# Reordering the opening of a conditional adapter with layer norm

## The chip, the cores and the metric

One core of one Trainium2 chip. The metric is the device time of one launch in microseconds (us).

## The reference

For each of 128 batches x is 128 x 512 in float32, and an index names one of 10 languages with its own weights:

```python
h = relu(einsum('bsh,bha->bsa', x, W1[id]) + b1[id])       # 512 -> 128
y = x + einsum('bsa,bah->bsh', h, W2[id]) + b2[id]          # 128 -> 512
normed = (y - mean(y)) * rsqrt(var(y) + 1e-5)
out = x + normed * gamma[id] + beta[id]
```

## The kernel before

A batch is one tile, 128 rows on the partitions. x is loaded in groups of four batches, in the opening in pairs (`load_part`, L86). For each batch:

- TensorE transposes x in four blocks (`transpose_x`, L264, the matmuls at L271), into one PSUM buffer; ScalarE copies them to SBUF (`copy_xT`, L273).
- TensorE multiplies with W1 (`down`, L290, eight half-matmuls at L294); ScalarE applies b1 and relu (`relu`, L300). Batches 0 to 16 get their W1 by a load of their own into a staging buffer (`load_first`, L158, pool `wp`); later ones get it from the resident `w1` by a ScalarE copy (`stage_w1`, L259). The resident `w1` arrives in four pieces of 640 KB (`load_w1`, L101).
- TensorE multiplies with W2 (`up`, L304, at L311) into one of five PSUM buffers (pool `p_y`). W2 is resident, loaded in two pieces.
- b2 is added in one of three ways. By TensorE, as a product of a picked row ahead of `up` (L310, batches in `b2_by_matmul`). By VectorE, in place (`vector_b2`, L318, batches in `b2_by_vector`). Else by GpSimd (POOL), which makes x + b2 ahead of time (`add_b2`, L277).
- VectorE adds x and sums (`residual`, L323), ScalarE squares and sums (`square`), small steps give the reciprocal deviation, VectorE scales by gamma (`scale`) and adds x + beta (`finish`, L399), which POOL has made ahead of time in the output buffer (`add_beta`, L283, pool `op`). SP stores two batches at a time (`store`).

The rows of beta, gamma and b2 must stand on all 128 partitions. There are 30 of them, numbered 0 to 9 for beta, 10 to 19 for gamma, 20 to 29 for b2. Each is dealt out in one of two ways: `spread` (L225), a TensorE product with a picked column and a ScalarE copy, or `shuffle_rows` (L244), a VectorE shuffle out of one tile that holds all of them. `spin` (L518) issues TensorE products whose result is not used.

The order on each engine is written out by hand: `keep` chains each instruction to the one before it on its engine. SP's queue issues the loads in the order written at L167 to L202. The opening is the list at L533 to L574, and the loop over `i` behind it takes the batches from there.

Of the kernel before, what the change touches and what calls it, by code (L numbers as in the profile page):

```python
# [26 lines left out]
def cond_resid_kernel(ctx: ExitStack, tc: tile.TileContext, x, itok, W1, b1, W2, b2, gamma, beta, out):  # L27
# [8 lines left out]
    nc = tc.nc  # L36
    B, S, H = x.shape
# [8 lines left out]
    def keep(ins):  # L46

        engine = ins.ins.engine
        if engine in last:
            tc.add_manual_dep(ins.ins, last[engine], behind, reason="kept order")  # L50
        last[engine] = ins.ins.name
        return ins
# [1 line left out]
    const = ctx.enter_context(tc.tile_pool(name="const", bufs=1))  # L54
    xp = ctx.enter_context(tc.tile_pool(name="xp", bufs=4))
    rp = ctx.enter_context(tc.tile_pool(name="rp", bufs=4))
    op = ctx.enter_context(tc.tile_pool(name="op", bufs=8))
    tp = ctx.enter_context(tc.tile_pool(name="tp", bufs=2))
    wp = ctx.enter_context(tc.tile_pool(name="wp", bufs=7))
    st = ctx.enter_context(tc.tile_pool(name="st", bufs=6))  # L60
    p_x = ctx.enter_context(tc.tile_pool(name="p_x", bufs=1, space=PSUM))
    p_h = ctx.enter_context(tc.tile_pool(name="p_h", bufs=1, space=PSUM))
# [4 lines left out]
    E = B - 5  # L67
# [18 lines left out]
    def load_part(lo, hi, engine=nc.sync):  # L86
        dst = xs[lo // G][:, lo % G : lo % G + hi - lo, :]
        keep(engine.dma_start(out=dst, in_=x[lo:hi].rearrange("b s h -> s b h")))
# [12 lines left out]
    def load_w1(k):  # L101
        keep(
            nc.sync.dma_start(out=w1[:, :, k, :], in_=W1[:, k * P : (k + 1) * P, :].rearrange("l p a -> p l a"))
        )
# [35 lines left out]
    def lid(b, engine):  # L140
        g = b // G
        if (g, engine) not in lids:
            loads, vals = nc.values_load_multi_w_load_instructions(
                lang[0:1, g * G : (g + 1) * G],
                engines=[engine],
                min_val=0,
                max_val=L - 1,
                skip_runtime_bounds_check_because="clamped on the chip to 0..L-1 above",
            )
            for ins in loads:  # L150
                keep(ins)
            lids[g, engine] = vals
        return lids[g, engine][b % G]
# [4 lines left out]
    def load_first(b):  # L158
        w1s[b] = wp.tile([P, KC, A], FP, tag="w1s", name=f"w1s_{b}")
        src = W1[bass.ds(lid(b, ET.SP), 1)].rearrange("o (p k) a -> p (o k a)", k=KC)  # L160
        keep(nc.sync.dma_start(out=w1s[b].rearrange("p k a -> p (k a)"), in_=src))  # L161
# [13 lines left out]
    load_part(4, 6)  # L175
    load_first(4)
    load_first(5)
    load_part(6, 8)
    load_first(6)
    load_first(7)  # L180
    xs[2] = xp.tile([P, G, H], FP, tag="x", name="x_2")
    load_part(8, 10)
    load_first(8)
    load_first(9)
    load_part(10, 12)
    load_first(10)
    load_first(11)
    xs[3] = xp.tile([P, G, H], FP, tag="x", name="x_3")
    load_part(12, 14)
    load_first(12)  # L190
    load_w1(0)
    load_first(13)
    load_part(14, 16)
    load_first(14)
    load_w1(1)
    load_first(15)
    xs[4] = xp.tile([P, G, H], FP, tag="x", name="x_4")
    load_part(16, 18)
    load_w1(2)
    load_first(16)  # L200
    load_part(18, 20)
    load_w1(3)  # L202

    def upper(lo):

# [19 lines left out]
    def spread(r, copier):  # L225
        t = (beta_b, gamma_b, b2_b)[r // L]
        row = p_y.tile([P, H], FP, tag="y", name=f"row_{r}")
        pick_r = pick[:, r : r + 1].to_broadcast([96, P])
        keep(nc.tensor.matmul(row, lhsT=pick_r, rhs=parts[:96, :], start=True, stop=True))  # L229
        dst = t[:, r % L * H : (r % L + 1) * H]  # L230
        if copier is nc.scalar:
            keep(nc.scalar.copy(dst, row))
        else:
            keep(nc.vector.tensor_copy(dst, row))
# [9 lines left out]
    def shuffle_rows(lo, hi):  # L244
        for r in range(lo, hi):
            t = (beta_b, gamma_b, b2_b)[r // L]
            keep(nc.vector.stream_shuffle(t[:, r % L * H : (r % L + 1) * H], fours[0], [r] * 32))  # L247
# [3 lines left out]


    def b2_by_matmul(b):
        return b in (0, 1) or b >= B - 2

    def b2_by_vector(b):
        return b in (2, 3, 9, 13, 17, 21) or 24 <= b < B - 8 and (b % 16 in (1, 6, 11) or b % 32 == 30)

    def stage_w1(b):  # L259
        w1s[b] = wp.tile([P, KC, A], FP, tag="w1s", name=f"w1s_{b}")  # L260
# [22 lines left out]
    def add_beta(b):  # L283
        g, j = divmod(b, 2)
        if j == 0:
            os[g] = op.tile([P, 2, H], FP, tag="o", name=f"o_{g}")
        v = lid(b, ET.Pool)
        keep(nc.gpsimd.tensor_tensor(os[g][:, j, :], xb(b), beta_b[:, bass.ds(v * H, H)], ALU.add))  # L288
# [15 lines left out]
    def up(b):  # L304
        v = lid(b, ET.PE)
        ys[b] = p_y.tile([P, H], FP, tag="y", name=f"py_{b}")
        m = b2_by_matmul(b)
        if m:
            pick_b = pick[:, bass.ds(v + 2 * L, 1)].to_broadcast([96, P])
            keep(nc.tensor.matmul(ys[b], lhsT=pick_b, rhs=parts[:96, :], start=True, stop=False))  # L310
        keep(nc.tensor.matmul(ys[b], lhsT=hT[b], rhs=w2[:, bass.ds(v * H, H)], start=not m, stop=True))  # L311
        del hT[b]
# [97 lines left out]
    def on(b):  # L410
        return 0 <= b < B
# [106 lines left out]
    def spin(n, width):  # L518
        idle = p_s.tile([P, H], FP, tag="s", name="idle")
        for _ in range(n):  # L520
            keep(
                nc.tensor.matmul(
                    idle[:, :width], lhsT=ones, rhs=ones[:, 0:1].to_broadcast([P, width]), start=True, stop=True
                )
            )
# [3 lines left out]
    def x_turn(b):  # L529
        transpose_x(b)  # L530
        copy_xT(b)
# [1 line left out]
    spin(7, H)  # L533
    four_copies()
    spread(10, nc.scalar)
    spin(1, H)
    x_turn(0)
    transpose_b1()
    spread(11, nc.scalar)
    for n in (0, G):  # L540
        lid(n, ET.PE)
    shuffle_rows(0, 10)
    x_turn(1)
    spread(12, nc.scalar)
    spread(13, nc.scalar)
    down(0)
    relu(0)
    spread(14, nc.scalar)
    x_turn(2)
    spread(15, nc.scalar)  # L550
    down(1)
    relu(1)
    spread(16, nc.scalar)
    spread(17, nc.scalar)
    x_turn(3)
    down(2)
    relu(2)
    spread(18, nc.scalar)
    spread(19, nc.scalar)
    add_beta(0)  # L560
    add_beta(1)
    spread(20, nc.scalar)
    spread(21, nc.scalar)
    down(3)
    relu(3)
    spread(22, nc.scalar)
    add_beta(2)
    add_beta(3)
    shuffle_rows(23, 30)
    spin(1, H)  # L570
    spin(1, H // 2)
    up(0)
    x_turn(4)
    up(1)  # L574

    turned = 5
    for i in range(3, B + U):
        b = i - U - 1
        if b > G and b % G == 2 and b // G + 3 < NG and b // G + 3 >= 5:
            load_x(b // G + 3)  # L580
        up_to = i
        if b <= E:
            if turned <= up_to and on(turned):
                transpose_x(turned)
            add_b2(b + 2)
            if 4 <= b + 2 <= E:
                add_beta(b + 2)
        for n in range(turned, min(B, up_to) + 1):
            if on(n) and (n > turned or b > E):
                transpose_x(n)  # L590
            down(n - 1)
            if on(n):
                copy_xT(n)
            relu(n - 1)
            if on(n + 1) and n + 1 >= FIRST:
                stage_w1(n + 1)
        turned = max(turned, min(B, up_to) + 1)
        if i - U >= 2 and on(i - U):
            up(i - U)

        g, half = divmod(b, 2)
        p = g - 1
        mine, old = 0 <= p < B // 2, 0 <= p - 1 < B // 2
        if b == E:
            add_b2(b + 3)
            add_beta(b + 1)
            add_b2(b + 4)
            for n in range(b + 2, B):
                add_beta(n)
        if b > E:  # L610
            tail(b)
        elif half == 0:
            if on(b):
                vector_b2(b)
                residual(b)
                square(b)
            if mine:
                scale(2 * p)
                rstd(p, 1)
            if old:  # L620
                finish(2 * p - 1)
                store(p - 1)
        else:
            if on(b):
                vector_b2(b)
            if mine:
                rstd(p, 2)
            if on(b):
                residual(b)
                square(b)  # L630
            if mine:
                rstd(p, 3)
                scale(2 * p + 1)
            if mine:
                finish(2 * p)
        if 0 <= g and b <= E and half == 1:
            scalar_means(g)
            deviation(g)

        for n, engine in ((turned + 2, ET.Activation), (i - U + 3, ET.PE), (b + 1, ET.DVE), (b + 6, ET.Pool)):  # L640
            if on(n):
                lid(n, engine)
# [37 lines left out]
```

## Time and profile before

| what | us |
|---|---|
| median of 3 runs | 304.56 (304.44 to 304.68) |
| the profiled execution | 304.08 |
| its span | 302.3 |
| TensorE (PE) busy | 290.6 |
| VectorE (DVE) busy | 294.2 |
| ScalarE (ACT) busy | 279.6 |
| GpSimd (POOL) busy | 284.9 |

Times in the trace count from the start of the span. PEld is TensorE's weight load, SP the engine that issues most DMAs. Matmuls are pipelined: the distance from start to start tells more than the length shown.

### The profile page before, as it was taken

What the parts mean: (1) busy time and instruction counts of PE and PEld (TensorE: products, weight loads), DVE (VectorE), ACT (ScalarE), POOL (GpSimd) and SP (SyncE); (2) the same over time, 40 slices, a digit from 0 to 9 for tenths busy, and PEclk for the clock granted to TensorE, in tenths of its full rate; (3) what the DMA queues carried; (4) which work ended last, traced back from release to release, by engine and by line L of the source; (5) the groups of instructions that cost most, each with busy time, mean ns of one, the idle gap of its engine ahead of it and who ended that gap; (6) DMA issues with size and microseconds to landing.
All of it is one profiled execution on the core that took longest, in us unless ns stands there. A gap on an engine that the chain in (4) does not pass through costs nothing.

```text
span 302.3 us, 7001 instructions
## 1 busy us (share of the span) xinstructions
PE 290.6 (96%) x1820; PEld 218.0 (72%) x1821; DVE 294.2 (97%) x784; ACT 279.6 (92%) x771; POOL 284.9 (94%) x240
## 2 busy tenths in 40 slices
PE   7899999999999999999999999999999999999980
PEld 3758787777777777777777777777777777777740
DVE  6989999999999999999999999999999999999995
ACT  5878789999999999999999999999999999999982
POOL 1299998999999999999999999999999999999995
PEclk9999999999999999999999999999999999999997
DMA  6999999986667876766678667767866666882244
GB/s 235 385 389 364 346 339 402 404 307 206 233 234 243 279 255 205 244 209 261 222 280 270 212 204 240 263 226 261 279 211 221 218 253 217 271 283 113 108 166 173
DMA packets 43929, 77.33 MB, mean 256 GB/s; under 512 B 2121, under 2 KB 8020, under 8 KB 43890
## 3 DMA queue, kind: packets, MB, share of 16 engines
q1 hardware_dynamic: 43254, 76.31, 73.5%
q10 hardware_dynamic: 636, 0.57, 0.6%
q8 instruction: 15, 0.25, 0.3%
q14 instruction: 24, 0.20, 0.2%
HBM read 43.32 MB, written 33.55 MB: 254 GB/s over the span
## 4 chain that ended last, share of the span: by engine, by line
PE 89%; DVE 5%; DMA 2%; issue 1%; ACT 1%; SPq 0%; POOL 0%; DVEq 0%; ACTq 0%; POOLq 0%
PE ph L294 36%; PE py L311 35%; PE pxT L271 18%; DMA x<-in_x_dram 2%; DVE py L394 2%; DVE py L328 1%; DVE o L403 1%; PE row L229 1%; SPq L161 0%; ACT n L450 0%; ACT sq L351 0%; ACT sq L436 0%; DVE o L461 0%; ACT w1s L262 0%; DVE rstd L370 0%
## 5 line engine op out<-in xcount | busy, mean ns | idle before, releaser
L288 POOL TENSOR_TENSOR o<-x,beta_b 128x512 f32<-128x512 f32 x128 | 170.1, 1359 | 12.7 <-DVE beta_b L247 11.6
L294 PE MATMUL ph<-xT,w1s 128*128 128x128 f32 x1024 | 135.3, 275 | 0.2 <-DMA w1s<-in_L_cond_W_dram 0.2
L281 POOL TENSOR_TENSOR r<-x,b_b 128x512 f32<-128x512 f32 x97 | 131.7, 1360 | 0.0
L311 PE MATMUL py<-w,hT 128*128 x256 | 131.3, 595 | 0.0
L294 PEld LDWEIGHTS ph<-xT,w1s 128*128 128x128 f32 x1024 | 124.8, 192 | 1.3 <-issue 0.6
L271 PEld LDWEIGHTS pxT<-ident,x 128*128 128x128 f32 x512 | 66.0, 149 | 66.8 <-issue 49.9
L394 DVE SCALAR_TENSOR_TENSOR py<-py,nmean,gamma_b 128x512 f32<-128x512 f32 x126 | 94.8, 753 | 0.0
L403 DVE SCALAR_TENSOR_TENSOR o<-py,rstd,o 128x512 f32<-128x512 f32 x122 | 91.1, 747 | 0.0
L351 ACT ACTIVATE sq<-py,sum 128x512 f32<-128x512 f32 x124 | 85.8, 692 | 0.6 <-DVE py L328 0.6
L275 ACT COPY xT<-pxT 128x512 f32<-128x512 f32 x128 | 74.7, 583 | 4.3 <-PE pxT L271 4.1
L271 PE MATMUL pxT<-ident,x 128*128 128x128 f32 x512 | 77.6, 274 | 0.8 <-DMA x<-in_x_dram 0.6
L262 ACT COPY w1s<-w 128x512 f32 x111 | 68.0, 613 | 0.0
L328 DVE SCALAR_TENSOR_TENSOR py<-py,r 128x512 f32<-128x512 f32 x97 | 66.9, 690 | 0.2
L302 ACT ACTIVATE hT<-ph,b1T 128x128 f32<-128x128 f32 x128 | 46.9, 367 | 8.8 <-PE ph L294 4.2
L311 PEld LDWEIGHTS py<-w,hT 128*128 128x128 f32 x256 | 39.1, 192 | 1.4 <-issue 0.7
L351 ACT ACTIVATION_READ_ACCUMULATOR sq<-py,sum 128x1 f32 x124 | 25.1, 202 | 0.0
L328 DVE SCALAR_TENSOR_TENSOR py<-py,x 128x512 f32<-128x512 f32 x31 | 21.7, 699 | 1.4 <-PE py L311 1.1
L321 DVE TENSOR_TENSOR py<-py,b_b 128x512 f32<-128x512 f32 x27 | 18.6, 689 | 0.1
L361 ACT ACTIVATE root<-ssq,eps 128x2 f32<-128x2 f32 x62 | 16.5, 265 | 0.0
L328 DVE DVE_READ_ACCUMULATOR py<-py,r 128x1 f32 x97 | 13.6, 140 | 0.0
L342 ACT ACTIVATE nmean<-sum 128x2 f32<-128x2 f32 x62 | 12.3, 198 | 0.0
L365 DVE SCALAR_TENSOR_TENSOR part<-ssq,root 128x2 f32<-128x2 f32 x62 | 9.3, 149 | 0.2 <-ACT root L361 0.2
(57 smaller groups left out, 81.2 us busy)
## 6 DMA issues: line engine op xcount, KB each, us to landing
out_dram<-o SPq DMA_DIRECT2D x61, 512.0 KB, 3.3
x<-in_x_dram SPq DMA_DIRECT2D x27, 1024.0 KB, 6.7
x<-in_x_dram SPq DMA_DIRECT2D x10, 512.0 KB, 7.2
w1s<-in_L_cond_W_dram SPq DMA_DIRECT2D x17, 256.0 KB, 8.7
w<-in_L_cond_W_dram SPq DMA_DIRECT2D x4, 640.0 KB, 8.2
w<-in_L_cond_W_dram SPq DMA_DIRECT2D x1, 1792.0 KB, 9.8
w<-in_L_cond_W_dram SPq DMA_DIRECT2D x1, 768.0 KB, 5.3
out_dram<-o SPq DMA_DIRECT2D x3, 256.0 KB, 2.0
```

The costliest lines, as they stand in the source:

```text
L262: keep(nc.scalar.copy(w1s[b].rearrange("p k a -> p (k a)"), src))
L271: keep(nc.tensor.transpose(pxs[b][:, k, :], cols, ident))
L275: keep(nc.scalar.copy(xT[b], pxs.pop(b)))
L281: keep(nc.gpsimd.tensor_tensor(rs[b], xb(b), b2_b[:, bass.ds(v * H, H)], ALU.add))
L288: keep(nc.gpsimd.tensor_tensor(os[g][:, j, :], xb(b), beta_b[:, bass.ds(v * H, H)], ALU.add))
L294: nc.tensor.matmul(phs[b], lhsT=w1s[b][:, k, :], rhs=xT[b][:, k, :], start=(k == 0), stop=(k == KC - 1))
L302: keep(nc.scalar.activation(hT[b], phs.pop(b), AF.Relu, bias=b1T[:, bass.ds(lid(b, ET.Activation), 1)]))
L311: keep(nc.tensor.matmul(ys[b], lhsT=hT[b], rhs=w2[:, bass.ds(v * H, H)], start=not m, stop=True))
L328: nc.vector.scalar_tensor_tensor(ys[b], ys[b], 1.0, r, ALU.mult, ALU.add, accum_out=col(sums, b))
L351: nc.scalar.activation(sq, ys[b], AF.Square, bias=col(sums, b), scale=-float(H), accum_out=col(ssqs, b))
L394: nc.vector.scalar_tensor_tensor(ys[b], ys[b], col(nmeans, b), gamma_b[:, bass.ds(v * H, H)], ALU.add, ALU.mult)
L403: nc.vector.scalar_tensor_tensor(o, ys.pop(b), rstds[g][:, j : j + 1], o, ALU.mult, ALU.add)
```

## The change

Six things are changed.

- In the opening `up(0)` and `up(1)` stand together, ahead of the transposes of batch 4. Before, those stood between them.
- Batch 0 gets its b2 by VectorE and no longer by TensorE; of batches 9 and 10, batch 10 now gets it by VectorE and 9 by POOL.
- The 30 rows are dealt out anew: before, beta by shuffles, gamma by spreads; now both kinds are mixed, with 14 spreads in place of 13 and 16 shuffles in place of 17. The idle products stand elsewhere, three wide and two half ones in place of two wide and one half one, besides the first seven.
- `add_beta` of batches 0 to 4 is issued in the opening, at other places.
- The loads behind W2 stand in another order. `load_first(6)` is ahead of x of 6 and 7; the first piece of the resident `w1` comes right behind that, ahead of `load_first(7)`; and so on.
- The pool `wp` has five buffers in place of seven, the pool `op` nine in place of eight.

```diff
-    op = ctx.enter_context(tc.tile_pool(name="op", bufs=8))
+    op = ctx.enter_context(tc.tile_pool(name="op", bufs=9))
-    wp = ctx.enter_context(tc.tile_pool(name="wp", bufs=7))
+    wp = ctx.enter_context(tc.tile_pool(name="wp", bufs=5))
...
     load_part(4, 6)
     load_first(4)
     load_first(5)
+    load_first(6)
     load_part(6, 8)
-    load_first(6)
+    load_w1(0)
     load_first(7)
+    load_first(8)
     xs[2] = xp.tile([P, G, H], FP, tag="x", name="x_2")
     load_part(8, 10)
-    load_first(8)
+    load_part(10, 12)
     load_first(9)
-    load_part(10, 12)
-    load_first(10)
-    load_first(11)
+    load_w1(1)
     xs[3] = xp.tile([P, G, H], FP, tag="x", name="x_3")
     load_part(12, 14)
+    load_first(10)
+    load_part(14, 16)
+    load_first(11)
     load_first(12)
-    load_w1(0)
-    load_first(13)
-    load_part(14, 16)
-    load_first(14)
-    load_w1(1)
-    load_first(15)
     xs[4] = xp.tile([P, G, H], FP, tag="x", name="x_4")
     load_part(16, 18)
+    load_first(13)
     load_w1(2)
+    load_first(14)
+    load_first(15)
     load_first(16)
+    load_w1(3)
     load_part(18, 20)
-    load_w1(3)
...
     def b2_by_matmul(b):
-        return b in (0, 1) or b >= B - 2
+        return b in (1,) or b >= B - 2
     def b2_by_vector(b):
-        return b in (2, 3, 9, 13, 17, 21) or ...
+        return b in (0, 2, 3, 10, 13, 17, 21) or ...
...
     spread(10, nc.scalar)
-    spin(1, H)
+    shuffle_rows(9, 10)
+    spread(0, nc.scalar)
     x_turn(0)
     transpose_b1()
...
     relu(3)
-    spread(22, nc.scalar)
+    shuffle_rows(26, 27)
+    spread(28, nc.scalar)
+    spread(16, nc.scalar)
+    spread(18, nc.scalar)
+    shuffle_rows(27, 28)
+    up(0)
+    shuffle_rows(21, 22)
+    shuffle_rows(25, 26)
+    shuffle_rows(20, 21)
+    up(1)
+    x_turn(4)
     add_beta(2)
     add_beta(3)
-    shuffle_rows(23, 30)
-    spin(1, H)
-    spin(1, H // 2)
-    up(0)
-    x_turn(4)
-    up(1)
+    add_beta(4)
+    shuffle_rows(24, 25)
```

More of the change, by code (lines that the diff above doesn't have):

```diff
@@ L253, in b2_by_matmul @@
     def b2_by_matmul(b):
-        return b in (0, 1) or b >= B - 2
+        return b in (1,) or b >= B - 2
     def b2_by_vector(b):
-        return b in (2, 3, 9, 13, 17, 21) or 24 <= b < B - 8 and (b % 16 in (1, 6, 11) or b % 32 == 30)
+        return b in (0, 2, 3, 10, 13, 17, 21) or 24 <= b < B - 8 and (b % 16 in (1, 6, 11) or b % 32 == 30)
     def stage_w1(b):
@@ L535, in cond_resid_kernel @@
     spread(10, nc.scalar)
-    spin(1, H)
+    shuffle_rows(9, 10)
+    spread(0, nc.scalar)
     x_turn(0)
     transpose_b1()
-    spread(11, nc.scalar)
+    shuffle_rows(5, 6)
+    spin(1, H)
     for n in (0, G):
         lid(n, ET.PE)
-    shuffle_rows(0, 10)
+    shuffle_rows(4, 5)
+    shuffle_rows(6, 7)
+    shuffle_rows(2, 3)
+    spread(17, nc.scalar)
+    spread(1, nc.scalar)
     x_turn(1)
-    spread(12, nc.scalar)
-    spread(13, nc.scalar)
+    spread(11, nc.scalar)
     down(0)
     relu(0)
-    spread(14, nc.scalar)
+    shuffle_rows(13, 14)
+    spread(3, nc.scalar)
+    spread(12, nc.scalar)
+    shuffle_rows(7, 8)
+    spread(8, nc.scalar)
+    add_beta(0)
+    add_beta(1)
     x_turn(2)
-    spread(15, nc.scalar)
+    spin(2, H)
+    spin(1, H // 2)
+    shuffle_rows(14, 15)
     down(1)
     relu(1)
-    spread(16, nc.scalar)
-    spread(17, nc.scalar)
+    shuffle_rows(29, 30)
+    spin(1, H // 2)
+    shuffle_rows(23, 24)
+    spread(15, nc.scalar)
     x_turn(3)
@@ L557, in cond_resid_kernel @@
     relu(2)
-    spread(18, nc.scalar)
+    spread(22, nc.scalar)
     spread(19, nc.scalar)
[L560 to L563, printed above, removed]
     down(3)
     relu(3)
-    spread(22, nc.scalar)
+    shuffle_rows(26, 27)
[9 more added lines that the diff above has]
+    x_turn(4)
     add_beta(2)
     add_beta(3)
-    shuffle_rows(23, 30)
-    spin(1, H)
-    spin(1, H // 2)
-    up(0)
-    x_turn(4)
-    up(1)
+    add_beta(4)
+    shuffle_rows(24, 25)
     turned = 5
@@ L580, in cond_resid_kernel @@
             load_x(b // G + 3)
-        up_to = i
+        up_to = i + {}.get(i, 0)
         if b <= E:
@@ L585, in cond_resid_kernel @@
             add_b2(b + 2)
-            if 4 <= b + 2 <= E:
+            if 5 <= b + 2 <= E:
                 add_beta(b + 2)
```

## The prediction

> **What bounds the kernel now.** I read the page first, then TensorE's time by stretches, its timeline where the change sits, and last the landings of the loads.
>
> ```profile
> span 302.3 us, 7001 instructions
> PE 290.6 (96%) x1820; PEld 218.0 (72%) x1821; DVE 294.2 (97%) x784; ACT 279.6 (92%) x771; POOL 284.9 (94%) x240
> PE 89%; DVE 5%; DMA 2%; issue 1%; ACT 1%; SPq 0%; POOL 0%; DVEq 0%; ACTq 0%; POOLq 0%
> 20.00:25.00 5.00, 5.00 (x34) 4.06 (x33) 4.88 (x14) 4.39 (x14) 5.00 (x5) 1.00 1.05 384
> 100.00:150.00 50.00, 50.00 (x321) 37.88 (x320) 49.93 (x131) 49.01 (x140) 50.00 (x42) 1.00 0.73 244
> ```
>
> Four engines are nearly full, so busy shares do not choose between them. The chain that ended last does: 89% of it is PE. In the stretches (length, busy time of PE, PEld, DVE, ACT and POOL, granted clock, DMA share, GB/s) PE has no gap from 20 us on. So whatever moves PE's unbroken stretch moves the end by as much, if the others keep up. The second reading is the DMA share: 1.05 at 20 to 25 us against 0.73 later. In the opening the DMA engines have no slack either, and there the order of the loads is the order of their landing. The span is 302.3 us in an execution of 304.08 us; the median of the runs shown is 304.56. I take differences inside the profiled execution and add them to the median.
>
> **The products up of 0 and 1.** I call the four transposes of a batch its turn (L271), L294 its product down, L311 its product up. PE's timeline (start, length) around the exchanged steps, the wait in it, and ACT's copy of turn 4:
>
> ```profile
> 16.15 0.38 PE L310 MATMUL py<-parts,pick 96*128 96x512 bf16 x1
> 16.37 1.10 PE L311 MATMUL py<-w,hT 128*128 x2
> 17.47 0.75 PE L271 MATMUL pxT<-ident,x 128*128 128x128 f32 x4
> 18.05 0.38 PE L310 MATMUL py<-parts,pick 96*128 96x512 bf16 x1
> 18.27 1.88 PE L311 MATMUL py<-w,hT 128*128 x4
> 19.99 0.63 PE L271 MATMUL pxT<-ident,x 128*128 128x128 f32 x4
> 20.46 1.06 PE L294 MATMUL ph<-xT,w1s 128*128 128x128 f32 x8
> 21.35 1.02 PE L311 MATMUL py<-w,hT 128*128 x2
> PEld pxT L271 <- DMA x<-in_x_dram: 0.8, 1, 0.8
> 18.31 0.59 ACT L275 COPY xT<-pxT 128x512 f32<-128x512 f32 x1 [1.53 <-PE pxT L271]
> ```
>
> By starts (lengths are pipelined) a product up takes (19.99 - 18.27) / 2 = 0.86, the b2 row ahead of it 16.37 - 16.15 = 0.22, a turn 20.46 - 19.99 = 0.47, but 18.05 - 17.47 = 0.58 when it had to wait for its data, since its weight loads are then not hidden. Turn 4 waited for x of batch 4. Now up(0), without a row, stands there: it starts between 16.15 and 16.37, and I take 16.20. Then 0.86, row 1 with 0.22, up(1) 0.86, turn 4 0.47, up(2) 0.86 give 19.47 for turn 5. But turn 5 also needs the copy of turn 4, which started 18.31 - 17.47 = 0.84 after the turn and took 0.59: 18.14 + 1.43 = 19.57. Against 19.99 that gains about 0.40, with ends at 0.25 and 0.55. If nothing else stood in the way, that would be the result.
>
> **b2 of batch 0, the rows, POOL.**
>
> ```profile
> 19.40 0.70 DVE L328 SCALAR_TENSOR_TENSOR py<-py,x 128x512 f32<-128x512 f32 x1 [1.08 <-PE py L311]
> 13.10 4.98 POOL L288 TENSOR_TENSOR o<-x,beta_b 128x512 f32<-128x512 f32 x4 [11.64 <-DVE beta_b L247]
> 91.01 0.75 DVE L403 SCALAR_TENSOR_TENSOR o<-py,rstd,o 128x512 f32<-128x512 f32 x1
> 91.81 1.12 PE L311 MATMUL py<-w,hT 128*128 x2
> ```
>
> VectorE's new addition for batch 0 costs about 0.70, like its neighbours, and fits into its 1.08 idle ahead of residual(1): nothing. Moving the vector batch from 9 to 10 is not quite free. VectorE falls behind by one such step and recovers within the next batches; one place later, it begins 13, 17 and 21 a little later. At 91 us the cover is gone already: finish ends at 91.01 + 0.75 = 91.76, and the product up that takes the freed buffer begins at 91.81 and lasts 1.12 instead of 1.02. I take another 0.10 there, bounds 0 and 0.25.
>
> POOL idled 11.64 for the beta rows; with rows 0, 1, 3 and 8 by ACT they are ready earlier. Nothing waits for POOL's first sums, so that gains 0, and so does the ninth output buffer. PE gets one row and one and a half idle products more before 16 us, at 0.22 for each full one some 0.55, under its waits for x and W2; were that cover gone, turn 5 would come up to 0.55 later, which the next part would swallow.
>
> **The loads.** All go through SP's queue and land in that order. Between the load of W1 of batch 5 (called f5; the pair x8-9 likewise) and turn 8 the order was x6-7, f6, f7, x8-9, f8. Now it is f6, x6-7, w1(0), f7, f8, x8-9: a 640 KB piece of the resident W1, ahead of turn 8's data. Issue rows of SP (start, length) with, below each, its size and the us to landing, then PE's own turn 8 and down(7):
>
> ```profile
> 8.79 0.47 SPq L161 DMA_DIRECT2D w1s<-in_L_cond_W_dram  x1
> w1s<-in_L_cond_W_dram SPq DMA_DIRECT2D x1, 256.0 KB, 10.0
> 16.20 0.33 SPq L161 DMA_DIRECT2D w1s<-in_L_cond_W_dram  x1
> w1s<-in_L_cond_W_dram SPq DMA_DIRECT2D x1, 256.0 KB, 8.7
> 18.11 0.39 SPq L88 DMA_DIRECT2D x<-in_x_dram  x1
> x<-in_x_dram SPq DMA_DIRECT2D x1, 512.0 KB, 8.8
> 28.21 0.99 SPq L161 DMA_DIRECT2D w1s<-in_L_cond_W_dram  x1
> w1s<-in_L_cond_W_dram SPq DMA_DIRECT2D x1, 256.0 KB, 7.1
> 29.26 0.54 SPq L103 DMA_DIRECT2D w<-in_L_cond_W_dram  x1
> w<-in_L_cond_W_dram SPq DMA_DIRECT2D x1, 640.0 KB, 8.2
> 26.65 0.63 PE L271 MATMUL pxT<-ident,x 128*128 128x128 f32 x4
> 27.12 0.28 PE L294 MATMUL ph<-xT,w1s 128*128 128x128 f32 x1
> ```
>
> The rows are f5, f8, x10-11, f14 and w1(1). f8, the last of the old group, landed at 16.20 + 8.7 = 24.90. The new group holds the same 1792 KB plus w1(0), and x8-9 is its last: it lands at 24.90 plus the time of one w1 piece. That time stands in the next two: f14 landed at 35.31, w1(1) right behind it at 37.46, so 2.15. x8-9 lands at 24.90 + 2.15 = 27.05.
>
> Turn 8 stood at 26.65 and would come at 26.25 with the gain. So it waits. What it pays beyond the landing:
>
> ```profile
> 3.76 0.37 SPq L161 DMA_DIRECT2D w1s<-in_L_cond_W_dram  x1
> w1s<-in_L_cond_W_dram SPq DMA_DIRECT2D x1, 256.0 KB, 4.2
> 8.09 1.13 PE L294 MATMUL ph<-xT,w1s 128*128 128x128 f32 x8 [0.16 <-DMA w1s<-in_L_cond_W_dram]
> ```
>
> f0 landed at 7.96 and its product began at 8.09, 0.13 later. Turn 8 thus begins at 27.18, takes 0.58 as turn 4 did after its wait, and down(7) begins at 27.76 instead of 27.12: 0.64 late. Queued behind it on PE are down(7) and up(6), whose data is there, and so the whole rest. Later turns have their x early again: x10-11 follows x8-9 directly and turn 10 is two batches away.
>
> The sum: the gain of 0.40 is eaten by the wait, which sets PE 0.64 late; VectorE adds 0.10; together +0.74. In the profiled execution 304.08 becomes 304.82; from the median, **305.3**. If the opening gained more or less, turn 8 would not move.
>
> **What the landings hide.** From f5 (18.79) to f8 (24.90) 1792 KB took 6.11; from f8 to x10-11 (26.91) 768 KB took 2.01, 0.67 for each 256 KB. At that pace 6.11 should have been 4.69. So 1.42 was lost in that stretch. What else ran there, and the packets under W1 pieces:
>
> ```profile
> q8 instruction: 1, 0.02, 5.7%
> DMA packets 236, 0.46 MB, mean 384 GB/s; under 512 B 18, under 2 KB 18, under 8 KB 235
> DMA packets 359, 0.19 MB, mean 299 GB/s; under 512 B 1, under 2 KB 352, under 8 KB 359
> ```
>
> The first two rows are of 21.5 to 22.7 us, the third of 29.2 to 29.85. One transfer of instructions ran on the same engines; a load has landed only when its slowest engine is through, so I put the 1.42 down to that. PE has only two instructions more ahead of it (a row and two idle products in, a b2 row with its address steps out), so I expect the transfer at nearly the same place, before x8-9. The Trainium skill (Runtime: NRT & Kernel Launch, Instruction fetch mechanics) says that engines refill instructions in 16 KiB blocks by a DMA queue of their own and that the cost is mostly hidden; the trace agrees on the size. By its word on the cost alone the 1.42 would not be there, and the result would be that of the first rival.
>
> W1 pieces are packets under 2 KB (352 of 359) at 299 GB/s, against 384 for whole rows; 640 KB at 299 GB/s would be 2.19, near the 2.15 that I use. At the pace of whole rows it would be 2.5 x 0.67 = 1.68. Bounds for w1(0): 1.68 and 2.19. The Trainium skill (DMA: Bandwidth & Descriptors, Specifications) gives 512 B as the least transfer at line rate, which speaks for the first; the row speaks against it.
>
> **Rivals.**
>
> *x8-9 is in time, and the kernel gets faster.* The place is the same wait. If the instruction transfer falls behind x8-9, or on an engine with less to do, x8-9 lands at 27.05 - 1.42 = 25.63, ahead of 26.25. Then -0.40 + 0.10 = -0.30: 304.3. It decides when x8-9 lands before 26.12. For it: the transfer's time is known from one execution only. Against: it would have to move by some four us. Chance 0.16.
>
> *W1 pieces go at the pace of whole rows.* x8-9 lands at 24.90 + 1.68 = 26.58, down(7) begins at 26.58 + 0.13 + 0.58 = 27.29, +0.17, with VectorE +0.27: 304.8. Against it stands the direct pair f14, w1(1). Chance 0.08.
>
> *The five staging buffers starve the loads.* f9 and later now wait for down(4) and later, and SP's queue holds x and w1 behind them. After x8-9 come x10-11, f9, w1(1), x12-13, f10: 6 x 0.67 + 2.15 = 6.17, so f10 lands at 33.22; down(10) comes at 27.76 + 3 x 2.22 = 34.42 (2.22 being (26.65 - 19.99) / 3). That leaves 1.2. It decides when the halts of SP's queue leave the engines dry for longer than that; with a halt as long as one w1 piece, 2.15, f10 is 0.95 late and the result is 306.2. Against it: the DMA share of 1.05 says that there is a backlog. Chance 0.08.
>
> **How the numbers follow.** The forecast has 0.68. Its own range: 304.96 with neither hand-over nor uncovered loads nor VectorE's term (27.05 - 26.65 = +0.40), up to 306.0 if a second, half as large instruction transfer (0.7) meets the same engine. The range 304.2 to 305.9 takes in the first two rivals and leaves out the third and the thin ends. About 0.2% or 0.61 us is what a measurement of this kernel can tell from no change. Of the forecast's 0.68 some seven tenths lie above +0.61 (0.48) and the rest within (0.20); the third rival lies above (0.08), the second within (0.08), the first within (0.11) but for an opening that gains more than my bound of 0.55 (0.05). So faster 0.05, same 0.39, slower 0.56.
>
> **What would show it.** Right: PE's turn of batch 8 waits about 0.9 for x, and down(7) begins near 27.8; up(0), up(1), turn 4 stand without a gap from 16.2 to 18.6; the L310 row is there once in the opening; the steps after keep their pitch. Wrong: turn 8 without a wait, or x8-9 landing before 26; PE waiting for staged W1 at down(9) to down(12); a wait of PE for ACT or VectorE ahead of 20 us; or a pitch between 30 and 90 us that differs from before.

## The result and the profile after

| | before | after |
|---|---|---|
| median of 22 runs each, us | 304.43 (304.01 to 304.68) | 304.88 (304.45 to 305.37) |
| ratio after / before | | 1.0017 [1.0012, 1.0023] |
| the profiled execution, us | 304.08 | 304.97 |
| its span, us | 302.3 | 303.2 |

The change costs time: 0.45 us between the medians, 0.89 us between the two profiled executions. The ratio lies inside the 0.2% that the prediction called no change; its interval reaches over that bound and does not hold 1.

The page of the kernel after: span, busy time by engine, and the engines' shares of the chain that ended last.

```profile
span 303.2 us, 7005 instructions
PE 291.4 (96%) x1823; PEld 217.7 (72%) x1823; DVE 294.1 (97%) x783; ACT 280.1 (92%) x772; POOL 285.2 (94%) x240
PE 86%; DVE 5%; DMA 5%; issue 1%; ACT 1%; SPq 1%; POOL 0%; DVEq 0%; ACTq 0%; POOLq 0%
```

The busy times hardly moved. The chain did: 5% of it is now DMA, against 2%, and 3% of 303.2 us is one load. PE's timeline of the kernel after (start, length) shows where it is:

```profile
16.26 1.04 PE L311 MATMUL py<-w,hT 128*128 x2
17.14 0.38 PE L310 MATMUL py<-parts,pick 96*128 96x512 bf16 x1
17.36 1.02 PE L311 MATMUL py<-w,hT 128*128 x2
18.22 0.63 PE L271 MATMUL pxT<-ident,x 128*128 128x128 f32 x4
18.69 1.02 PE L311 MATMUL py<-w,hT 128*128 x2
19.59 0.74 PE L271 MATMUL pxT<-ident,x 128*128 128x128 f32 x4
20.17 1.06 PE L294 MATMUL ph<-xT,w1s 128*128 128x128 f32 x8
...
25.50 1.02 PE L311 MATMUL py<-w,hT 128*128 x2
27.45 0.72 PE L271 MATMUL pxT<-ident,x 128*128 128x128 f32 x4 [0.92 <-DMA x<-in_x_dram]
28.00 1.06 PE L294 MATMUL ph<-xT,w1s 128*128 128x128 f32 x8
```

The opening now has up(0), one b2 row, up(1), turn 4, up(2) without a gap, as forecast, and down(4) begins at 20.17 instead of 20.46: 0.29 gained. Then turn 8 waits 0.92 us for x8-9, and down(7) begins at 28.00 instead of 27.12: 0.88 late. The span is 0.9 longer, so everything behind that point keeps the lateness and adds nothing.

The landings around it: SP's issues of f5 and f8 (start, length; below each its size and the us to landing), and the chain of waits at the same place, from the issue of x8-9 on (start, length, what).

```profile
9.21 0.36 SPq L161 DMA_DIRECT2D w1s<-in_L_cond_W_dram  x1
w1s<-in_L_cond_W_dram SPq DMA_DIRECT2D x1, 256.0 KB, 9.6
18.29 0.36 SPq L161 DMA_DIRECT2D w1s<-in_L_cond_W_dram  x1
w1s<-in_L_cond_W_dram SPq DMA_DIRECT2D x1, 256.0 KB, 7.7
18.69 8.62 DMA x<-in_x_dram
27.31 0.14 issue
```

f5 lands at 18.81, as before; f8 at 25.99; x8-9 at 18.69 + 8.62 = 27.31, and turn 8 begins 0.14 later.

### The profile page after: what moved, and what is told of

Its sections match the earlier page's. It is cut to its first block, busy times and chain, and to the rows that moved or that the text cites. A ratio compares the mean times of both kernels' runs of the same rounds, so it can differ in the third digit from the quotient of the medians.

```text
span 303.2 us, 7005 instructions
## 1 busy us (share of the span) xinstructions
PE 291.4 (96%) x1823; PEld 217.7 (72%) x1823; DVE 294.1 (97%) x783; ACT 280.1 (92%) x772; POOL 285.2 (94%) x240
## 4 chain that ended last, share of the span: by engine, by line
PE 86%; DVE 5%; DMA 5%; issue 1%; ACT 1%; SPq 1%; POOL 0%; DVEq 0%; ACTq 0%; POOLq 0%
PE ph L294 35%; PE py L311 33%; PE pxT L271 17%; DMA x<-in_x_dram 5%; DVE py L394 2%; DVE py L328 1%; DVE o L403 1%; PE row L229 0%; SPq L161 0%; PE idle L522 0%; ACT n L450 0%; ACT sq L351 0%; ACT sq L436 0%; DVE o L461 0%; ACT w1s L262 0%
## 5 line engine op out<-in xcount | busy, mean ns | idle before, releaser
L288 POOL TENSOR_TENSOR o<-x,beta_b 128x512 f32<-128x512 f32 x128 | 168.2, 1338 | 11.1 <-ACT beta_b L232 9.6
L281 POOL TENSOR_TENSOR r<-x,b_b 128x512 f32<-128x512 f32 x97 | 129.8, 1340 | 0.0
L321 DVE TENSOR_TENSOR py<-py,b_b 128x512 f32<-128x512 f32 x28 | 19.3, 689 | 1.4 <-PE py L311 1.4
```

What stands on the lines that cost most here:

```text
L281: keep(nc.gpsimd.tensor_tensor(rs[b], xb(b), b2_b[:, bass.ds(v * H, H)], ALU.add))
```

## The experiments

Three questions: is the whole loss the place of w1(0) ahead of x8-9; what is the opening worth without it; and is it the instruction transfer that slows the stretch from f5 to f8? Two more came up on the way. Each kernel was timed beside before on the same chip; before's median differs a little from chip to chip, so each comparison names the one that was taken with it.

**Loads alone (loads_only).** Before, with the block of loads and the two pools of after:

```diff
-    op = ctx.enter_context(tc.tile_pool(name="op", bufs=8))
+    op = ctx.enter_context(tc.tile_pool(name="op", bufs=9))
-    wp = ctx.enter_context(tc.tile_pool(name="wp", bufs=7))
+    wp = ctx.enter_context(tc.tile_pool(name="wp", bufs=5))
...
+    load_first(6)
     load_part(6, 8)
-    load_first(6)
+    load_w1(0)
     load_first(7)
+    load_first(8)
...
     load_part(8, 10)
...
```

> The kernel before with only the new order of the loads and the new pools (five staging buffers, nine output buffers); the opening's work as before. Theory: turn 8 begins when x of 8 and 9 has landed, near 27.4, as in the changed kernel, whatever PE did earlier; time +0.88 in the profiled execution and +0.5 in the timed runs, as with the whole change. Rival (the work dealt out anew in the opening, b2 on VectorE or the rows cost the time): no slower than the kernel before, ratio 1.000.

Measured: 304.87 (304.56 to 305.15) against 304.35, ratio 1.0014 [1.0005, 1.0023]; profiled 304.87. PE's turn 8 and down(7) in it:

```profile
27.32 0.72 PE L271 MATMUL pxT<-ident,x 128*128 128x128 f32 x4 [0.49 <-DMA x<-in_x_dram]
27.87 1.06 PE L294 MATMUL ph<-xT,w1s 128*128 128x128 f32 x8
```

Down(7) comes within 0.13 of where it does after the whole change, though the opening is that of before. The wait is shorter (0.49 against 0.92) by about what the old opening is later. So the loads make the loss, and it needs nothing of the new opening.

**w1(0) behind x8-9 (w1_behind_x89).** After, with one line moved:

```diff
     load_part(6, 8)
-    load_w1(0)
     load_first(7)
     load_first(8)
     xs[2] = xp.tile([P, G, H], FP, tag="x", name="x_2")
     load_part(8, 10)
+    load_w1(0)
     load_part(10, 12)
```

> The changed kernel with one load moved: the first piece of the resident W1 goes behind x of 8 and 9 instead of ahead of it. Theory (the change loses its time in the wait of turn 8, because that piece stands ahead of x of 8 and 9): the wait of 0.92 us is gone, turn 8 stands near 26.36 and down(7) near 26.83, the opening's gain of 0.29 stays, and the time is 0.3 below the kernel before (ratio 0.999). Rival (the slowest DMA engine is late by itself, whatever is ahead): turn 8 still waits 0.5 us or more, and the time stays above that of the kernel before. Second rival (later loads are short because of the five staging buffers): the wait goes from turn 8 to a later batch and the time is as in the changed kernel.

Measured: 304.62 (304.09 to 305.48) against 304.35, ratio 1.0007 [0.9997, 1.0017]; profiled 304.18. PE's turn 8 and down(7), then turns 11 and 12 with the products down between:

```profile
26.60 0.63 PE L271 MATMUL pxT<-ident,x 128*128 128x128 f32 x4
27.07 1.06 PE L294 MATMUL ph<-xT,w1s 128*128 128x128 f32 x8
...
33.26 0.63 PE L271 MATMUL pxT<-ident,x 128*128 128x128 f32 x4
33.75 1.13 PE L294 MATMUL ph<-xT,w1s 128*128 128x128 f32 x8
35.58 0.64 PE L271 MATMUL pxT<-ident,x 128*128 128x128 f32 x4
```

The wait is gone and down(7) is 0.93 earlier than after the change; the profiled execution is 0.79 shorter. The order of these two loads is the cause of the wait.

The opening's gain was expected to stay, and it did not: down(7) is only 0.05 ahead of before's 27.12, where 0.29 was expected. Turn 2 shows why, in before, after and this run:

```profile
10.07 0.72 PE L271 MATMUL pxT<-ident,x 128*128 128x128 f32 x4 [0.63 <-DMA x<-in_x_dram]
10.03 0.72 PE L271 MATMUL pxT<-ident,x 128*128 128x128 f32 x4 [0.21 <-DMA x<-in_x_dram]
10.28 0.72 PE L271 MATMUL pxT<-ident,x 128*128 128x128 f32 x4 [0.44 <-DMA x<-in_x_dram]
```

It waits for its x in all three, and here x came 0.25 later than in after. From turn 2 to turn 4 the new opening takes 18.22 - 10.03 = 8.19 in after and 18.45 - 10.28 = 8.17 here, so a late x goes through to the end.

From turn 11 to turn 12 it is 2.32, where the kernel before has 2.22: 0.10 lost at down(10), the place named by the third rival. But the DMA share stays between 1.04 and 1.15 from 18 to 38 us, read in steps of 2, so the engines did not run dry, as that rival has it. In the new order f10 stands behind w1(1). Its landing is not on record; an estimate from f9's (21.48 + 8.0 = 29.48) with 2.15 and 3 x 0.67 behind it is 33.64, and down(10) begins at 33.75. In the kernel after that place shows nothing, since PE is late there by more.

The median, 304.62, is not below before's, although the profiled execution is. The next run says why in part.

**The opening alone (opening_only and opening_only_again).** After, with before's block of loads and its eight and seven buffers.

> The changed kernel with the old order of the loads and the old pools; only the opening's work is new. Theory: turn 8 does not wait, down(7) begins 0.3 earlier than in the kernel before (26.83 instead of 27.12), and the time is 0.3 us less (ratio 0.999), unless a later load takes it back: x of 20 to 23 is the one I would look at. Rival (the opening's new work costs): ratio 1.001 or more.

Measured: 304.65 (304.03 to 305.3) against 304.35, ratio 1.0008 [0.9998, 1.0018]; the profiled execution was its lowest, 304.03. That did not fit: no load is in the way, and yet its runs spread over 1.3 us, while 28 of the 29 of before beside it lie between 304.12 and 304.75 (one is at 305.31). I profiled the same kernel again:

> The kernel with only the opening's work new, looked at once more. Turn 2 to turn 4 takes 8.17 again. If this execution is a late one, the clock's full grant comes later than 4.9 us and the turns of batches 0 and 1 are late by as much as the end; if it is an early one, they are at 5.4 and 7.0 again.

That execution took 305.02. PE's timeline in the first profile (two row products, turn 0, turn 2, turn 4, turn 5, down(7)):

```profile
5.00 0.59 PE L229 MATMUL row<-parts,pick 96*128 96x512 bf16 x2
5.43 0.63 PE L271 MATMUL pxT<-ident,x 128*128 128x128 f32 x4
...
10.21 0.72 PE L271 MATMUL pxT<-ident,x 128*128 128x128 f32 x4 [0.25 <-ACT beta_b L232]
...
18.38 0.63 PE L271 MATMUL pxT<-ident,x 128*128 128x128 f32 x4
...
19.75 0.75 PE L271 MATMUL pxT<-ident,x 128*128 128x128 f32 x4
...
27.00 1.06 PE L294 MATMUL ph<-xT,w1s 128*128 128x128 f32 x8
```

and in the second, the same steps but the last:

```profile
5.17 1.06 PE L229 MATMUL row<-parts,pick 96*128 96x512 bf16 x2
6.02 1.06 PE L271 MATMUL pxT<-ident,x 128*128 128x128 f32 x4
...
11.37 0.63 PE L271 MATMUL pxT<-ident,x 128*128 128x128 f32 x4
...
19.45 0.63 PE L271 MATMUL pxT<-ident,x 128*128 128x128 f32 x4
...
20.81 0.75 PE L271 MATMUL pxT<-ident,x 128*128 128x128 f32 x4
```

The same products take twice the time at first: two rows 6.02 - 5.17 = 0.85 from start to start against 0.43. Turn 2 is 1.16 later, and turn 5 still 1.06 later: from turn 2 to turn 4 it is 8.17 in one and 8.08 in the other, so the new opening has nothing in between that would give way. In before that distance is 17.47 - 10.07 = 7.40 and ends with a wait for x of batch 4, of 17.47 - (16.37 + 0.86) = 0.24. So with the clock there the opening gained 0.29 at down(4) in after and, with turn 2 at 10.21, 0.13 here (20.33 against 20.46); when the clock comes late it loses about 1 us.

**An earlier instruction transfer (fetch_earlier).** After, with 32 idle products of 8 columns, so that PE's instructions run out sooner:

```diff
     relu(0)
+    spin(32, 8)
```

> The changed kernel with 32 more idle products of 8 columns on PE behind relu of batch 0: 64 more PE instructions, a few us of PE's slack. If the loss of 1.4 to 1.6 us between the landings of batch 5's and batch 8's W1 comes from the transfer of PE's instructions, that transfer moves some five us ahead (to about 16 or 17 us instead of 21.8), the W1 of batch 5 lands 1.4 later (near 20.2 instead of 18.83), the stretch between the two landings shrinks from 7.14 to about 5.7, and x of 8 and 9 lands as before (27.3), so that turn 8 stays at 27.45 and the time within 0.1 of the changed kernel. If the loss comes from the W1 piece or from the queue, the W1 of batch 5 lands at 18.83 as before and the stretch stays 7.1.

Measured: 306.02 (305.86 and 306.17), ratio 1.0049 [1.0031, 1.0068]. The time missed the expectation by far: in the profile the full clock came late here too, and with the idle products, 0.81 of PE's time, turn 5 stood at 21.61, so that turn 8, at 28.39, had no wait at all. What the landings say does not hang on that. SP's issues of f5 and f8 as above, and the row of the instruction queue from 18 to 19.2 us:

```profile
10.90 0.36 SPq L161 DMA_DIRECT2D w1s<-in_L_cond_W_dram  x1
w1s<-in_L_cond_W_dram SPq DMA_DIRECT2D x1, 256.0 KB, 9.4
18.81 0.74 SPq L161 DMA_DIRECT2D w1s<-in_L_cond_W_dram  x1
w1s<-in_L_cond_W_dram SPq DMA_DIRECT2D x1, 256.0 KB, 7.0
q8 instruction: 1, 0.02, 5.7%
```

The transfer began at 18.09 instead of 21.76. f5 landed at 20.3, 1.5 later than in after, and from f5 to f8 it took 25.81 - 20.3 = 5.5 instead of 7.2 us, for the same 1920 KB. The 1.5 us moved with the transfer, from the loads behind f5 to f5 itself; so it is the transfer that costs them. f5 was also issued 1.7 later here than in after, since its staging buffer waits for down(0); that is not the reason, for in the next run it is issued at 10.61, nearly as late, and lands at 18.81.

**W1 in rows of 2 KB (w1_rows_2k).** The pieces of W1 are cut by language instead of by block of 128 rows, so that each packet carries 2 KB; x is transposed in interleaved columns for all batches to fit. The first piece has 768 KB, three of ten languages.

```diff
-EARLY = 17
+EARLY = 128
...
+        lo, hi = (0, 3, 5, 8, 10)[k : k + 2]
         keep(
-            nc.sync.dma_start(out=w1[:, :, k, :], in_=W1[:, k * P : (k + 1) * P, :].rearrange("l p a -> p l a"))
+            nc.sync.dma_start(
+                out=w1[:, lo:hi].rearrange("p l k a -> p l (k a)"),
+                in_=W1[lo:hi].rearrange("l (p k) a -> p l (k a)", k=KC),
+            )
         )
```

> The changed kernel with the resident W1 loaded in pieces of whole languages by rows of 2 KB (3, 2, 3, 2 languages) and with the transposes of all batches in the strided form that fits them, which costs 0.03 for each batch after 17, some 3.3 us over the run: only the opening is to be read. The first piece is 768 KB instead of 640. If the packet of 512 B is what makes a piece dear, 768 KB take 2.0 instead of 2.15 to 2.2, x of 8 and 9 lands 0.15 to 0.2 earlier, and turn 8 begins near 27.25. If 512 B go at line rate, 768 KB take a fifth longer, 2.6, and turn 8 begins near 27.9.

Measured: 307.55, a single execution. Its time says nothing of the pieces: the clock came late in this profile too, so that turn 8 (27.29) did not wait, and the interleaved columns make PE's weight loads 10 us longer over the span. The landings do. First the packets of after between 21.5 and 22.5 us, in the middle of w1(0):

```profile
DMA packets 475, 0.32 MB, mean 316 GB/s; under 512 B 15, under 2 KB 432, under 8 KB 474
```

then those of w1_rows_2k between 20 and 23 us, and its f5 and f8:

```profile
DMA packets 602, 1.16 MB, mean 386 GB/s; under 512 B 43, under 2 KB 43, under 8 KB 601
10.61 0.35 SPq L165 DMA_DIRECT2D w1s<-in_L_cond_W_dram  x1
w1s<-in_L_cond_W_dram SPq DMA_DIRECT2D x1, 256.0 KB, 8.2
16.75 0.36 SPq L165 DMA_DIRECT2D w1s<-in_L_cond_W_dram  x1
w1s<-in_L_cond_W_dram SPq DMA_DIRECT2D x1, 256.0 KB, 8.9
```

From f5 to f8 it took 25.65 - 18.81 = 6.8, against 7.2, though 128 KB more lay in between: that is 8 x 0.67, all at the pace of whole rows, and 1.5 for the transfer. It is the short packets that make a piece of W1 dear. The Trainium skill (DMA: Bandwidth & Descriptors, Specifications) has 512 B as enough for line rate; this row pair does not agree.

**No idle products behind turn 2 (no_late_idle), nine at the start (nine_first_idle).** Both are opening_only with one thing changed. The first takes out the three late calls of `spin`, to give the opening slack again:

```diff
     x_turn(2)
-    spin(2, H)
-    spin(1, H // 2)
...
     shuffle_rows(29, 30)
-    spin(1, H // 2)
```

> The kernel with only the opening's work new (loads and pools as before), less the idle products behind the turn of batch 2 (two wide, two half). Its median was 0.3 above the kernel before although its profiled execution was 0.05 below. Theory (the new opening has no slack between the landing of x of 2 and 3 and up(0), 8.17 us from turn 2 to turn 4 in every profile, so that any late start of PE goes through to the end): 0.6 us of idle products less gives that slack; turn 4 stays near 18.2, the times no longer reach 305, and the median is 0.2 to 0.3 below the kernel before. Rival (the spread comes from the loads or from later on): median and spread as with the idle products, 304.6 and 304.0 to 305.3. Second rival: without them TensorE's clock drops, the granted clock shows it, and the time rises.

The second keeps PE busy until the first row products are ready:

```diff
-    spin(7, H)
+    spin(9, H)
```

> The kernel with only the opening's work new, with nine wide idle products at the start in place of seven. If the late starts come from TensorE's clock, which was full at 4.2 to 4.8 us in five profiles and only at 9.86 in one, a busy stretch without a gap up to the first product makes late starts rarer: fewer of the twelve times above 304.9, median 304.3 or less. If not, the times are as with seven, or 0.3 us later since the first product waits.

Measured, both against 304.30: 304.02 (303.81 to 304.7), ratio 0.9992 [0.9983, 1.0001], and 304.02 (303.74 to 306.0), ratio 0.9995 [0.9983, 1.0007]. Eleven of the twelve runs with nine idle products are at 304.43 or below; one is at 306.0. Without the late idle products up(0) waits:

```profile
16.52 1.10 PE L311 MATMUL py<-w,hT 128*128 x2 [0.97 <-ACT gamma_b L232]
```

The row names ACT's copy of a gamma row, which had long been done; W2's second piece landed at 16.4 in that trace, and up(0) needs it; the wait is put down to that. So 0.97 us of slack stands ahead of up(0), and a late clock of about 1 us would fit into it. Turn 4 stood at 18.53 and not near 18.2 as expected, so the time of this profile (304.1) is no better than before's. Either edit brings the median 0.6 below opening_only's (on another chip, with before at 304.30 against 304.35), to where its quickest executions are.

**Both, and a control (nine_and_no_late, before_nine).** The first is no_late_idle with `spin(9, H)`, the second is before with `spin(9, H)`.

> The new opening with the old loads and pools, nine wide idle products at the start and none behind the turn of batch 2: the two edits that each gave 304.02 against 304.30. Theory (both only take away what a late clock costs, the one by rarer late clocks, the other by slack): together hardly more than each, 0.25 to 0.4 below the kernel before, with no time above 304.5. Rival (they act on different things): 0.5 or more below it. Up(0) cannot start before W2 has landed near 16.1 to 16.4.

> The kernel before with nine wide idle products at the start in place of seven. If the late clock costs the kernel before little, since its turn 4 waits for x of batch 4 anyway, its median stays within 0.1 of the kernel before. If the late clock costs any opening the same, it falls by 0.3, as the new opening did.

Measured, both against 304.25: 303.80 (303.63 to 304.19), ratio 0.9983 [0.9974, 0.9992], and 304.19 (304.08 to 304.3), ratio 0.9998 [0.9989, 1.0007]. Before's median gains nothing from the longer start, but its spread shrinks: eleven runs within 304.08 to 304.30, beside 21 of before with seven idle products from 304.03 to 305.1. So before seems to pay for a late clock too, only less. An estimate: in the late profile of opening_only down(0) began at 9.75, 1.56 later than in the other; before has 10.07 - (9.06 + 0.22) = 0.79 of slack ahead of turn 2 and 0.24 ahead of turn 4, which leaves some 0.5 late. No late execution of before was profiled.

The median of the new opening with before's loads, nine idle products and no late ones lies 0.45 below before's, and none of its runs comes near 304.9, the median of after. Its profile does not show where the 0.45 is: that execution took 304.02, the second longest of the eleven, and its down(7) is at 27.06, 0.06 ahead of before's.

## Why the prediction was right

Its mechanism (x8-9 late behind w1(0), and turn 8 waits) is what happened; the median of 304.88 lies in its range, 0.42 below its number of 305.3. By its own bound of 0.61 us the 0.45 between the medians counts as no change, to which it gave 0.39, against 0.56 for slower. Point by point:

- **Turn 8 waits for x8-9, and that is the loss.** Shown: the row of turn 8 names it, loads_only has the loss by itself, and w1_behind_x89 is rid of it. The first rival (x8-9 in time) did not occur: the instruction transfer began at 21.76, against 21.54 before, nearly the same place, as the prediction said from the few instructions that PE has more.
- **The landing: 27.05 predicted, 27.31 measured.** The undersized term is the 1.42 that the transfer costs. From f5 to f8 it took 7.2; by the prediction's own prices, 0.67 for each 256 KB and 2.15 for w1(0), it should be 5 x 0.67 + 2.15 = 5.5. So 1.7 was lost, not 1.42, and that is the 0.26. The transfer itself took 1.19 us in this trace and 1.09 before. x8-9 followed f8 by 1.32, and 2 x 0.67 was assumed.
- **W1's piece at 2.15.** The second rival (1.68, the pace of whole rows) fell: fetch_earlier, with nothing else in the stretch, needs 5.5 where 5 x 0.67 + 2.15 gives 5.5, and w1_rows_2k shows that the packets are the reason.
- **Hand-over and uncovered weight loads: 0.13 and 0.58 predicted,** 0.14 and 28.00 - 27.45 = 0.55 measured.
- **The opening's gain: 0.40 predicted, 0.29 at down(4).** Turn 5 came at 19.59, where 19.57 was predicted. But it waited there for ACT's copy (its first weight load waits 0.70, to 19.58), so its own weight loads were not hidden: it took 20.17 - 19.59 = 0.58 instead of 0.47. The prediction knew that price and applied it to turn 8 alone. It changed nothing in the end, as the prediction said it would not, since turn 8 waits in any case.
- **VectorE's 0.10 did not come.** Here the prediction was wrong. Turns 37 and 38 of PE, around the place where it was to be paid, first in before, then in after:

```profile
90.45 0.60 PE L271 MATMUL pxT<-ident,x 128*128 128x128 f32 x4
92.77 0.60 PE L271 MATMUL pxT<-ident,x 128*128 128x128 f32 x4
```

```profile
91.34 0.60 PE L271 MATMUL pxT<-ident,x 128*128 128x128 f32 x4
93.66 0.60 PE L271 MATMUL pxT<-ident,x 128*128 128x128 f32 x4
```

  The distance is 2.32 in both, and the lateness is 0.89 at both turns. So nothing more was paid here; where VectorE made up its later steps was not followed.
- **Five staging buffers, the third rival.** It had a margin of 1.2 by the prediction and did not bite in after. With turn 8's wait gone 0.10 is lost at down(10), but with the engines busy throughout; by the estimate above f10 is late behind w1(1).
- **POOL's earlier rows gained nothing,** as said: POOL's share of the chain is 0% in both.

So in the profiled executions the prediction has +0.74 and the measurement +0.89: the landing was 0.26 short, VectorE 0.10 too much. That the sum is near owes a little to these two going opposite ways.

What the prediction did not have is how executions differ. It took the profiled difference over to the medians, and those differ by 0.45 only. Before's profiled execution, 304.08, lies 0.35 below its median; after's, 304.97, 0.09 above. One part can be argued from the runs: a late clock costs opening_only about 1 us, and with after's loads most of that would pass in the wait of turn 8, since 27.59, where turn 8 stood in the late execution of opening_only, is only 0.14 behind the 27.45 of after. Before would pay some 0.5 in a late execution by the estimate above. But nine idle products lowered its median by only 0.06, after's runs spread too, from 304.45 to 305.37, and no second execution of before or after was profiled, so the 0.44 between the two differences stays open.

## What to carry to other kernels

When loads land in the order of issue and the queue has no slack, price a load that is moved forward by the first consumer of whatever it overtakes: one 640 KB piece ahead of an x pair cost all that a better opening had won, and more. Price short rows by their own landing, not by bytes. When a change packs an opening, look whether it took out a wait that also absorbed variation from run to run; profile a second execution before believing a gain of 0.3 us, and leave the slack where it costs nothing.

## What the hardware showed that was not expected

**When TensorE comes to full clock differs between executions of one kernel.** The clock records of the traces begin with full clock at 4.32 us in the first profile of opening_only and at 9.90 in the second; in after at 4.21, in fetch_earlier at 9.86, in w1_rows_2k at 9.27. The page's clock row hides it (it shows 9 for the first slice in both), and so does the mean granted clock (0.993 in fetch_earlier too); the lengths of the first products show it. The Trainium skill (TensorE: Matmul & The Clock Gate, What's actually happening) says that activity is watched in free-running windows of about 3.4 us and that the start of full clock therefore varies by some 0.5 us; the direction agrees, but here the two starts are 5.6 us apart. The first seven idle products run from 1.01 to 4.18, 3.17 us, and a gap of 0.61 follows; that nine of them make the late start rarer (one run of 12 is over 305, then none of 11, against four of 12 with seven) fits with a window that must be filled. On record full clock lasts 293.55 us in after and in the first profile of opening_only, 290.13 in fetch_earlier and 286.72 in the second of opening_only: steps of 3.42 and 3.41, so the changes do lie on such a grid. What fills a window no trace shows, and which runs were late is taken from their times alone, so the use of the nine is argued, not shown.

**One 16 KB instruction transfer delays the loads beside it.** It takes 1.1 to 1.2 us and 5.7% of the engines' time in a stretch of 1.2 us, which is one engine of 16 for that time, yet what is in the queue lands 1.4 to 1.7 us later. That a load waits for its slowest engine fits; the engines were not read one by one. The Trainium skill (Runtime: NRT & Kernel Launch, Instruction fetch mechanics) calls the cost of crossing a 16 KiB boundary mostly hidden. For the loads in this saturated stretch it is not: fetch_earlier moved the transfer by 3.7 us, and the loss went with it.
